# Four changes of order in the first half of a fused four-layer kernel: GpSimd's order by hand, the variance, the top-k rounds and two dense tiles

## The chip, the cores and the metric

The kernel is one program on one core of one Trainium2 chip. The metric is device time in microseconds (us) of that core, from one launch to its end; the figure for a kernel is the median over runs. Before the change three runs gave 838.84, 840.29 and 840.7 us, so a median of 840.29.

A core has five engines that run side by side, each with its own queue: TensorE (matrix products, PE in the profile), VectorE (DVE), ScalarE (ACT), GpSimd (POOL) and SyncE (SP), which here only starts transfers. An engine takes its instructions strictly in the order of its queue. One that waits for another engine holds up everything behind it.

## The reference, cut to what matters

The input x has 4 x 256 tokens of 256 values; ctx_512 has 4 x 256 rows of 64. Each of four layers adds a gated attention and a gated feed-forward part to x. The change touches layer 0, the attention of layer 1, and two things that are computed there ahead of time for later use: the ternary weights of layer 1's feed-forward part and the adjacency of layer 2.

```python
def _L0_xattn_ref(p, k_v, W_k, b_k, ln_gamma, ln_beta):
    kv = k_v @ W_k.T + b_k
    out = jnp.einsum('bij,bjd->bid', p, kv)
    sim = jnp.einsum('bid,bjd->bij', out, kv) * 256 ** (-0.5)
    mu = jnp.mean(sim, axis=-1, keepdims=True)
    var = jnp.var(sim, axis=-1, keepdims=True)
    sim = (sim - mu) * jax.lax.rsqrt(var + EPS) * ln_gamma + ln_beta
    return jax.nn.softmax(sim, axis=-1)

def _L0_ffn_ref(x, gate_w, gate_b, expert_w, expert_b):
    gate_logits = jnp.einsum('nsd,de->nse', x, gate_w) + gate_b
    _, top_idx = jax.lax.top_k(gate_logits, 2)                  # 2 of 8 experts
    all_out = jax.nn.relu(jnp.einsum('nsd,edo->nseo', x, expert_w) + expert_b)
    return jnp.take_along_axis(all_out, top_idx[..., None], axis=2).mean(axis=2)

# layer 1: causal softmax attention with 16 heads of 16 over keys from ctx_512;
# its feed-forward part rounds three 1024 x 256 weights to -1, 0 or 1:
def weight_quant(w):
    scale = 1.0 / jnp.clip(jnp.mean(jnp.abs(w)), EPS)
    return jnp.clip(jnp.round(w * scale), -1.0, 1.0) / scale

# layer 2's attention matrix comes from ctx_512 alone; k = 76 of 256
topk_vals = jax.lax.top_k(sim, k)[0]
sparse_mask = (sim >= topk_vals[:, :, -1:]).astype(sim.dtype)
A_learned = jax.nn.sigmoid(sim) * sparse_mask
A_learned = (A_learned + jnp.swapaxes(A_learned, -1, -2)) * 0.5

x = x + jnp.tanh(g_xattn[0]) * _L0_xattn_ref(_layernorm(x), ctx_512, ...)
x = x + jnp.tanh(g_ffn[0]) * _L0_ffn_ref(_layernorm(x), ...)
x = x + jnp.tanh(g_xattn[1]) * _L1_xattn_ref(_layernorm(x), ctx_512, ...)
...
```

## The kernel before, in words

**Tiles.** The 1024 tokens are eight tiles of 128 rows, which stay on chip all the time; a half is four tiles, two batch entries. A layernorm works on one half (`layernorm`, L173): statistics on VectorE, the power -0.5 of the variance on GpSimd (L183, ln_rstd), then four normalizations on VectorE (L187, xn). `transposed` (L193) turns the half on TensorE (L199) and copies it out (xnT, L109 when VectorE does it). `evac` (L105) gives such copies to VectorE and ScalarE by turns. `project` (L206) is the common matmul of projections and routing.

**The order.** Most of the kernel leaves the order of instructions to a scheduler. Up to the end of layer 1's attention TensorE's order is that of the source text (`in_order`, L217, opened at L444), and so are ScalarE's and VectorE's (L588 to L590, closed at L1034). GpSimd's is the scheduler's. SyncE starts the loads, each when its buffer is free. Matmuls write to eight PSUM banks that `bank` hands out in turn, so that an operation may have to wait until an earlier reader has left its bank.

**Layer 0, attention (L592 to L718).** For each half: the similarities (L634) on TensorE, with and without the layernorm's gain, their squares summed on ScalarE (L649, s_drop), the variance from them on VectorE (L654, s_ve) and its power on GpSimd (L656), then `softmax0` (L659: scaling at L660, maxima, Exp) and the gated addition `add0` (L680). The first half's normalization and the second half's similarities are interleaved; the routing of the first half ends the stage.

**Layer 0, feed-forward (L762 to L823).** All eight experts are computed for every token and multiplied by 0 or 0.5. `dense` does one tile: four banks, a bias matmul in each (L766), the experts' matmuls (L772), eight ReLUs on ScalarE that scale by the routing weight (L780, into buffers re, of which there are three), and the sum over experts on GpSimd (L785, L786). `add_mean` (L789) adds the result to x on VectorE. The loop runs over tiles 0 to 5; tile 6 and 7 are done in steps 0 and 1 of the next stage. Beside the tiles stand pieces of other work:

- top-k rounds for layer 2. A row's 76th largest value is found by ten rounds; each takes the eight largest (L479) and strikes them out (L482), the tenth applies the threshold (L486). There are 8 x 10 = 80 rounds, all on VectorE. `graph_rows(n)` (L493) puts the next n in the queue.
- keys and values of layer 1 (`keys1`, L516; `values1`, L531).
- four pieces for each of the three ternary weights (L549 to L571): `ternary_sum` of absolute values (ScalarE), `ternary_mean` (a matmul and three small operations on VectorE, L558 to L562), `ternary_scale` (L566 on ScalarE, L567 on VectorE) and `ternary_round` (ScalarE). The raw weights come through the same ten load buffers as the experts' weights.
- after tile 4, the layernorm of the first half for layer 1; the second half's is in step 3 of the attention.

**Layer 1, attention (L854 to L1033).** Per batch entry a query projection (`Maxima`, L206 with wq) and four steps that find each row's maximum (scores on TensorE, L885 m on VectorE, then two small operations and `late`, which adds the maxima to the queries); one batch entry later four steps (`Sums`) that compute exp(score - maximum) on ScalarE, multiply by the values, transpose (oT) and divide, then `turn` (attT) and `output` with the residual addition. So there are 20 steps and 5 more to drain; steps 4 to 15 do both kinds, steps 16 to 19 only sums. Top-k rounds and, from step 20 on, the transposition of the adjacency (`graph_batch`, L497) stand in these steps. Then follows layer 1's feed-forward part, whose first operation on VectorE is the quantization of its input (L1161).

How tiles, rounds and steps were written:

```python
means[t] = dense(t % HT, *((xt0, counts0) if t < HT else (xt1, counts1)))
graph_rows(3)
if t:
    add_mean(t - 1)
if t == 4:
    tiles = layernorm(0)
graph_rows((2, 6, 6, 6, 2, 4)[t])          # the loop, t = 0 to 5
...
if n < 2:                                  # the steps, n = 0 to 24
    means[6 + n] = dense(2 + n, xt1, counts1)
    add_mean(5 + n)
...
graph_rows(5 if n < 2 else 2)
```

## Time and profile before

| | us | what it is |
|---|---|---|
| median of three runs | 840.29 | without a profile |
| the profiled execution | 829.3 | one execution, recorded |
| its span | 827.6 | first to last instruction; 1.7 lies around it |
| PE, matmuls | 707.5 | 85% of the span |
| PEld, weight loads | 426.7 | 52%, beside matmuls |
| DVE | 510.6 | 62% |
| ACT | 283.3 | 34% |
| POOL | 212.2 | 26% |

The mean granted clock of TensorE in this execution is 0.914 of full speed. The profiled execution is shorter than each of the three runs, so sums over it are made against its own 829.3.

The parts of the span, with the time that the engines are busy in each and the clock (the parts that the prediction shows are left out):

| part of the span | what runs | length | PE | DVE | clock |
|---|---|---|---|---|---|
| 0 to 40.5 | loads, layer 0's attention, first half | 40.5 | 25.4 | 28.0 | 0.87 |
| 40.5 to 61.0 | its second half, first routing | 20.5 | 14.3 | 14.6 | 0.75 |
| 61.0 to 102.7 | dense tiles 0 to 4 | 41.7 | 41.7 | 35.0 | 0.92 |
| 262.3 to 360.0 | layer 1's feed-forward part | 97.7 | 73.6 | 80.1 | 0.92 |
| 360.0 to 827.6 | layers 2 and 3 | 467.6 | 424.5 | 234.0 | 0.94 |

Between them lie 102.7 to 123.9 (tile 5 and the layernorm for layer 1), 123.9 to 173.0 (dense tiles 6 and 7 with steps 0 to 3), 173.0 to 241.4 (steps 4 to 15) and 241.4 to 262.3 (the last steps).

How to read the lines that follow. In the busy slices each digit is the busy share of one of 40 equal slices in tenths. A line of waits says which instruction waits (engine, tile, line), what released it, and then total, number and longest of the waits in us. A line of the timeline begins with its time and its duration, both in us, then engine, line, operation, what is written and from what, the shape, and how many such instructions stand together; a bracket gives the wait ahead of it and what ended it. A line of windows gives a stretch, its length, each engine's busy time with its number of instructions, the clock, the share of the transfer engines and GB/s.

### The profile page before, as it was taken

The page shows a single profiled execution, that of the slowest core. Times are in us where ns is not written, and L with a number is a line of the kernel's source. Part 1 is how long each engine was busy: PE and PEld are TensorE (multiplying, and loading weights), DVE is VectorE, ACT ScalarE, POOL GpSimd, SP SyncE. Part 2 cuts the span into 40 slices and gives each one's busy share as a digit, 9 for nine tenths or more (in the row PEclk, how much of TensorE's full clock was granted, in tenths as well). Part 3 has the DMA queues.
Part 4 walks back from the last instruction along what each step waited for, and adds up shares of the span by engine and source line. Part 5 has one row for each costly group of instructions (what it writes and reads, how often), then busy time and mean ns, then how long its engine had stood idle before and what let it go on. Part 6 is the DMA issues. An engine that isn't in the chain of part 4 may idle for free.

```text
span 827.6 us, 11378 instructions
## 1 busy us (share of the span) xinstructions
PE 707.5 (85%) x4121; PEld 426.7 (52%) x4121; DVE 510.6 (62%) x1398; ACT 283.3 (34%) x583; POOL 212.2 (26%) x254
## 2 busy tenths in 40 slices
PE   5679939669989689729999997999998979989996
PEld 3434415446655367516477746654543325547754
DVE  6778883879885789864314455887777524213334
ACT  2444632423233143213103310156554655013320
POOL 4123352100000334210544362100000010733334
PEclk9778978779999799967999999899999998989998
DMA  8700111110000000000258833200000000369933
GB/s 256 252 0 1 38 38 30 49 37 2 20 2 8 13 1 1 0 0 1 85 182 284 271 95 108 84 1 2 1 1 2 1 1 0 113 238 333 341 108 109
DMA packets 32848, 64.35 MB, mean 78 GB/s; under 512 B 5180, under 2 KB 22488, under 8 KB 32536
## 3 DMA queue, kind: packets, MB, share of 16 engines
q1 hardware_dynamic: 24136, 31.47, 11.6%
q0 software_dynamic: 8224, 31.76, 11.5%
q8 instruction: 33, 0.54, 0.3%
q10 hardware_dynamic: 432, 0.39, 0.2%
q14 instruction: 23, 0.19, 0.1%
HBM read 49.31 MB, written 14.30 MB: 77 GB/s over the span
## 4 chain that ended last, share of the span: by engine, by line
PE 59%; DVE 19%; issue 10%; DMA 4%; ACT 4%; POOL 3%; SPq 0%; ACTq 0%; DVEq 0%; POOLq 0%
PE b L206 21%; PE b L772 6%; PE b L399 6%; PE b L1290 4%; PE b L1305 3%; PE b L1259 3%; PE b L347 3%; PE b L1106 3%; DVE pad L1266 3%; DMA d_w<-in_ffn_r_dram,d_of 2%; DVE xn L187 2%; POOL ln_rstd L183 2%; DVE x L372 2%; DVE g_work L482 1%; ACT pT L1297 1%
## 5 line engine op out<-in xcount | busy, mean ns | idle before, releaser
L206 PE MATMUL b<-xnT,w 128*128 128x512 f32 (+2 forms) x288 | 119.9, 574 | 10.4 <-DVE xnT L109 10.4
L1266 DVE TENSOR_REDUCE pad<-b 128x2 f32<-128x512 f32 x128 | 80.9, 684 | 20.7 <-PE b L1290 20.3
L206 PEld LDWEIGHTS b<-xnT,w 128*128 128x128 f32 (+1 forms) x288 | 56.3, 200 | 66.1 <-issue 62.5
L1297 ACT ACTIVATE pT<-b 128x512 f32<-128x512 f32 x128 | 68.7, 598 | 50.7 <-PE b L1290 50.7
L1259 PE MATMUL b<-kT,qT 32*128 32x256 f32 x512 | 71.8, 417 | 3.2 <-DVE pad L1266 3.2
L1290 PE MATMUL b<-qm,kT 32*128 32x512 f32 x256 | 73.6, 649 | 0.0
L312 POOL DMA_INDIRECT d_w<-in_ffn_r_dram,d_of x46 | 43.8, 952 | 109.1 <-PE b L319 61.5
L206 PE MATMUL b<-d_w,d_xT 128*128 128x256 f32 (+1 forms) x184 | 58.0, 439 | 2.8 <-DMA d_w<-in_ffn_r_dram,d_of 1.7
L772 PE MATMUL b<-w,xnT 128*128 128x512 f32 x128 | 59.9, 623 | 0.0
L1259 PEld LDWEIGHTS b<-kT,qT 32*128 32x128 f32 x512 | 41.7, 191 | 33.3 <-DVE pad L1266 10.9
L399 PE MATMUL b<-w,hT 128*128 128x256 f32 x224 | 53.9, 395 | 2.0 <-DVE hT L385 2.0
L785 POOL TENSOR_TENSOR re<-re 128x512 f32<-128x512 f32 (+1 forms) x32 | 32.4, 1015 | 75.1 <-ACT re L780 73.9
L384 ACT ACTIVATE sil<-b 128x512 f32<-128x512 f32 (+1 forms) x28 | 16.7, 597 | 99.7 <-PE b L206 99.7
L399 PEld LDWEIGHTS b<-w,hT 128*128 128x128 f32 x224 | 42.3, 195 | 15.0 <-issue 6.9
L385 DVE TENSOR_TENSOR hT<-b,sil 128x512 f32<-128x512 f32 (+1 forms) x28 | 19.3, 688 | 45.9 <-ACT sil L384 45.9
L183 POOL TENSOR_TENSOR ln_rstd<-ln_ve,neghalf 128x4 f32<-128x4 f32 x16 | 16.3, 1019 | 120.1 <-DVE ln_ve L181 120.0
L925 ACT ACTIVATE pT<-b 128x384 f32<-128x384 f32 x64 | 26.2, 497 | 53.7 <-PE b L919 53.7
L1106 PE MATMUL b<-had,zT 128*128 128x256 f32 x128 | 33.8, 421 | 10.3 <-ACT hwork L1117 7.2
L199 PE MATMUL b<-ident,xn 128*128 128x128 f32 x80 | 17.4, 359 | 29.1 <-DVE xn L187 28.0
L187 DVE TENSOR_SCALAR xn<-x,ln_mv,ln_rstd 128x256 f32<-128x256 f32 x64 | 26.5, 468 | 24.5 <-POOL ln_rstd L183 24.5
L772 PEld LDWEIGHTS b<-w,xnT 128*128 128x128 f32 x128 | 24.9, 200 | 31.0 <-issue 31.0
L885 DVE TENSOR_REDUCE m<-b 128x3 f32<-128x384 f32 x64 | 31.1, 547 | 13.9 <-PE b L879 13.9
(278 smaller groups left out, 1319.4 us busy)
## 6 DMA issues: line engine op xcount, KB each, us to landing
d_x<-rows_in SPq DMA_DIRECT2D x46, 128.0 KB, 4.4
rows_out<-d_y SPq DMA_DIRECT2D x46, 128.0 KB, 4.7
w<-in_ffn_s_dram SPq DMA_DIRECT2D x13, 384.0 KB, 3.5
w<-in_l_w_dram SPq DMA_DIRECT2D x6, 512.0 KB, 4.6
rows_in<-zero SPq DMA_DIRECT2D x1, 2944.0 KB, 14.3
w<-in_expert_w_dram SPq DMA_DIRECT2D x4, 512.0 KB, 5.6
x<-in_x_dram SPq DMA_DIRECT2D x8, 128.0 KB, 3.6
kT<-in_l_kT_dram SPq DMA_DIRECT2D x1, 1024.0 KB, 4.9
```

What stands on the lines that cost most here:

```text
L183: nc.gpsimd.tensor_tensor(rstd, ve, neghalf, ALU.pow)
L187: nc.vector.tensor_scalar(xn, x[h * HT + i], mv[:, i, 0:1], rstd[:, i : i + 1], ALU.subtract, ALU.mult)
L206: nc.tensor.matmul(dst, lhs(kc), rhs(kc), start=kc == 0, stop=kc == KC - 1)
L312: nc.gpsimd.indirect_dma_start(out=w, out_offset=None, in_=src, in_offset=self.indices(self.of[:, n : n + 1]))
L399: nc.tensor.matmul(po, hT[:hs, j, i * P : (i + 1) * P], w[:hs, 4 * hs : 4 * hs + D], start=j == 0, stop=j == len(ws) - 1,)
L772: nc.tensor.matmul(pe, xt[:, kc, i * P : (i + 1) * P], ws0[j][:, kc * 2 * D : (kc + 1) * 2 * D], start=False, stop=kc == KC - 1,)
L785: nc.gpsimd.tensor_add(re[:, :n, :], re[:, :n, :], re[:, n : 2 * n, :])
L1106: nc.tensor.matmul(pf[:, c // 2, (c % 2) * 2 * P : (c % 2 + 1) * 2 * P], self.zT[:, c0 : c0 + P], had2[:, n].rearrange("p s q -> p (s q)") ...
L1259: nc.tensor.matmul(pn[:, half * S : (half + 1) * S], self.qT[group(k), ah, g0 + half, qt * P : (qt + 1) * P], kT[group(k), ah, self.b * S ...
L1266: nc.vector.tensor_reduce(self.pads[qt][:, ah, g0 : g0 + 2, k, D3], pn.rearrange("p (g s) -> p g s", g=2), AX.X, ALU.max, negate=True,)
L1290: nc.tensor.matmul(pn, kT[group(k), ah, c : c + P], self.qm[group(k), ah, g0 : g0 + 2, :], start=True, stop=True)
L1297: nc.scalar.activation(self.pT[u][:, k, :], pn, AF.Exp, scale=D3**-0.5)
```

## The change

It leaves every operation in place and changes their order; the number of instructions of each engine is the same before and after.

- GpSimd's order becomes that of the source text too, for the same stretch as the others'. With it, the sum over experts is taken out of `dense` into a function of its own, `sum_up`, which stands after the statistics and the power for the layernorm in tile 4.
- The variance of the first attention's similarities is taken out of `similarities` into `factors`. For the second half it is called after `layernorm(0)`.
- The loads of the first raw ternary weight stand ahead of the experts' weights in SyncE's queue.
- The loop over tiles is unrolled: `ffn_tile(t, rounds, early)` does a tile, its sum, its rounds and its ternary pieces; keys and values follow in `part_of_keys(t)`. The pieces of the third ternary weight move from steps 2 to 4 of the attention to tiles 5 to 7.
- Dense tiles 6 and 7 leave steps 0 and 1: tile 6 stands ahead of the first query projection, tile 7 behind it, both ahead of step 0.
- The 80 rounds are placed anew. Tiles 0 to 5 had 5, 9, 9, 9, 5 and 7, steps 0 and 1 had 5 each, later ones 2. Now tiles 0 to 7 have 5, 9, 9, 8, 3, 7, 4 and 7, steps 0 to 3 none, steps 4 to 15 one each, and steps 16 to 19 four each. `graph_batch` moves one step later.

```diff
--- before.py
+++ after.py
@@ -154,6 +154,7 @@
     nc.sync.dma_start(rbias[:, 1, :], a["expert_bias"].partition_broadcast(P))
     ebias = const.tile([16, P], F32, tag="ebias", name="ebias")
     nc.sync.dma_start(ebias, a["expert_b"].rearrange("(p f) -> p f", p=16))
+    raw = [[weights(a["l1_w0"][j], FF1) for j in range(2)]]
     ws0 = [weights(a["expert_w"][j], KC * 2 * D) for j in range(E // 2)]
     had = const.tile([P, P], F32, tag="had", name="had")
     nc.sync.dma_start(had, a["hadamard"])
@@ -588,6 +589,7 @@
     all_orders = ExitStack()
     all_orders.enter_context(in_order(ACT))
     all_orders.enter_context(in_order(mybir.EngineType.DVE))
+    all_orders.enter_context(in_order(mybir.EngineType.Pool))
     with tc.tile_pool(name="l0a", bufs=1) as lp:
         tiles0 = layernorm(0)
         pk = bank()
@@ -650,11 +652,15 @@
                         drop[:, :S], sims[0][i][:, it, :], AF.Square,
                         accum_out=square[:, 2 * i + it : 2 * i + it + 1],
                     )
+            return sims[1], square
+
+        def factors(square):
             ve = sm([HT], "s0_ve")
             nc.vector.tensor_scalar(ve, square, 1.0 / (S * 256.0), 1e-6, ALU.mult, ALU.add)
             rstd = sm([HT], "s0_rstd")
             nc.gpsimd.tensor_tensor(rstd, ve, neghalf, ALU.pow)
-            return sims[1], rstd
+            return rstd
+
 
         def softmax0(pss, rstd, between=lambda: None):
             nc.vector.tensor_scalar_mul(rstd, rstd, 1.0 / 16.0)
@@ -699,21 +705,23 @@
         for j in range(E // 2):
             nc.sync.dma_start(eb[32 * j : 32 * j + 3, :], eb_parts[:, j * 2 * D : (j + 1) * 2 * D])
 
-        held = similarities(0, out_of(0, xt))
+        pss, square = similarities(0, out_of(0, xt))
+        rstd = factors(square)
         nc.scalar.activation(gates, gates, AF.Tanh)
         xt = transposed(tiles1)
         qkT2 = lp.tile([P, 2, 2, S], F32, tag="qkT2", name="qkT2")
         oT = []
-        weighted = softmax0(*held, lambda: oT.append(out_of(1, xt)))
+        weighted = softmax0(pss, rstd, lambda: oT.append(out_of(1, xt)))
         graph_projections(qkT2)
-        held = similarities(1, *oT)
+        pss, square = similarities(1, *oT)
         add0(0, *weighted)
         tiles0 = layernorm(0)
+        rstd = factors(square)
         graph_scores(0, qkT2)
         graph_scores(1, qkT2)
         xt0 = transposed(tiles0)
         pl = route(xt0, 0, E)
-        weighted = softmax0(*held)
+        weighted = softmax0(pss, rstd)
         counts0 = choose(pl)
         add0(1, *weighted)
 
@@ -780,9 +788,12 @@
                 nc.scalar.activation(
                     re[:, e % 4, :], pe[:, (e % 2) * D : (e % 2 + 1) * D], AF.Relu, scale=counts[:, i, e : e + 1]
                 )
-            if j % 2:
-                for n in (2, 1):
-                    nc.gpsimd.tensor_add(re[:, :n, :], re[:, :n, :], re[:, n : 2 * n, :])
+        return means
+
+    def sum_up(means):
+        for re in means:
+            for n in (2, 1):
+                nc.gpsimd.tensor_add(re[:, :n, :], re[:, :n, :], re[:, n : 2 * n, :])
         nc.gpsimd.tensor_add(means[0][:, 0, :], means[0][:, 0, :], means[1][:, 0, :])
         return means[0][:, 0, :]
 
@@ -791,36 +802,50 @@
 
     tiles1 = layernorm(1)
     wq = weights(a["l1_wq"], KC * 4 * P)
-    raw = [[weights(a[f"l1_w{n}"][j], FF1) for j in range(2)] for n in range(3)]
+    raw += [[weights(a[f"l1_w{n}"][j], FF1) for j in range(2)] for n in (1, 2)]
     means = {}
-    for t in range(NT - 2):
-        if t == 1:
-            pl = route(xt1, 0, E)
-        means[t] = dense(t % HT, *((xt0, counts0) if t < HT else (xt1, counts1)))
-        if t == 0:
-            nc.scalar.activation(
-                graph.rearrange("p t s -> p (t s)"), gsim.rearrange("p t s -> p (t s)"), AF.Sigmoid,
-                scale=1.0 / 16.0,
-            )
+
+    def ffn_tile(t, rounds, early=lambda: None):
+
+        parts = dense(t % HT, *((xt0, counts0) if t < HT else (xt1, counts1)))
         graph_rows(3)
-        if t == 1:
-            counts1 = choose(pl)
+        early()
         if t:
             add_mean(t - 1)
-        if t == 4:
-            tiles = layernorm(0)
-        graph_rows((2, 6, 6, 6, 2, 4)[t])
-        if t == 0:
-            xt1 = transposed(tiles1)
-        if t < HT:
-            keys1(t)
-            values1(*divmod(t, 2))
+        if t == HT:
+            tiles1.extend(layernorm(0))
+        means[t] = sum_up(parts)
+        graph_rows(rounds)
         for when, piece, n in (
             (0, ternary_sum, 0), (1, ternary_mean, 0), (1, ternary_scale, 0), (2, ternary_sum, 1),
             (2, ternary_round, 0), (3, ternary_mean, 1), (3, ternary_scale, 1), (4, ternary_round, 1),
+            (5, ternary_sum, 2), (6, ternary_mean, 2), (6, ternary_scale, 2), (7, ternary_round, 2),
         ):
             if t == when:
                 piece(n)
+
+    def part_of_keys(t):
+        keys1(t)
+        values1(*divmod(t, 2))
+
+    ffn_tile(0, 2)
+    nc.scalar.activation(
+        graph.rearrange("p t s -> p (t s)"), gsim.rearrange("p t s -> p (t s)"), AF.Sigmoid, scale=1.0 / 16.0
+    )
+    xt1 = transposed(tiles1)
+    part_of_keys(0)
+    pl = route(xt1, 0, E)
+    chosen = []
+    tiles1 = []
+    ffn_tile(1, 6, lambda: chosen.append(choose(pl)))
+    counts1, = chosen
+    part_of_keys(1)
+    ffn_tile(2, 6)
+    part_of_keys(2)
+    ffn_tile(3, 5)
+    part_of_keys(3)
+    ffn_tile(4, 0)
+    ffn_tile(5, 4)
 
 
 
@@ -989,24 +1014,16 @@
         with ExitStack():
             steps = 4 * (B + 1)
             plan = [([], []) for _ in range(steps + 5)]
-            xt = transposed(tiles)
+            ffn_tile(6, 1)
+            xt = transposed(tiles1)
             mx, sums, following = Maxima(0, xt), None, None
+            ffn_tile(7, 4)
+            add_mean(7)
+            in_l0f.close()
             for n in range(steps + 5):
                 b, j = divmod(n, 4)
-                if n < 2:
-                    means[6 + n] = dense(2 + n, xt1, counts1)
-                    add_mean(5 + n)
-                elif n == 2:
-                    add_mean(7)
-                    in_l0f.close()
-                    ternary_sum(2)
-                elif n == 3:
-                    ternary_mean(2)
-                    ternary_scale(2)
-                elif n == 4:
-                    ternary_round(2)
-                elif steps <= n < steps + B:
-                    graph_batch(n - steps)
+                if steps < n:
+                    graph_batch(n - steps - 1)
                 if j == 0 and 0 < n <= steps:
                     sums = Sums(b - 1, mx.qT) if n < steps else None
                     mx, following = following, None
@@ -1022,7 +1039,7 @@
                     if j == 3:
                         plan[n + 2][1].append(sums.turn)
                         plan[n + 3][1].append(sums.output)
-                graph_rows(5 if n < 2 else 2)
+                graph_rows(0 if n < 4 else 1 if n < 16 else 4)
                 for todo in plan[n][1]:
                     todo()
                 if n == 3:
```

## What was predicted

> **What bounds the kernel now.** I read the busy slices first, then TensorE's waits, then stage windows, then the timeline at each wait. The slices (20.7 us each):
>
> ```profile
> PE   5679939669989689729999997999998979989996
> DVE  6778883879885789864314455887777524213334
> PEclk9778978779999799967999999899999998989998
> ```
>
> TensorE is nearly full from slice 9 to the end of the attention and is hollow in slices 0 to 2, 5, 7 and 8; VectorE is high just there. TensorE's longest waits up to 300 us (total, times, longest) name it:
>
> ```profile
> PE b L199 <- DVE xn L187: 17.7, 8, 5.7
> PE b L206 <- DVE xnT L109: 11.7, 3, 8.4
> PE b L848 <- DVE m L885: 6.5, 6, 3.3
> ...
> PE b L897 <- DVE m L885: 3.4, 1, 3.4
> ```
>
> So the stretch from 0 to 173 us is set by VectorE's queue. The stages (length; busy time of PE, weight loads, DVE, ACT, POOL; clock):
>
> ```profile
> 102.70:123.90 21.20, 8.17 (x23) 3.62 (x21) 18.97 (x52) 7.76 (x18) 10.61 (x11) 0.72 0.13 37
> 123.90:173.00 49.10, 38.33 (x200) 21.97 (x200) 30.69 (x94) 17.27 (x33) 10.44 (x11) 0.78 0.16 49
> 173.00:241.40 68.40, 60.86 (x708) 40.58 (x708) 58.44 (x182) 20.06 (x49) 1.01 (x1) 0.97 0.02 7
> 241.40:262.30 20.90, 20.78 (x205) 12.78 (x204) 10.84 (x39) 9.06 (x23) 0.00 (x0) 0.92 0.01 2
> ```
>
> Read: VectorE full in the first row, TensorE full in the last, where VectorE has 10.06 us free. The points that the change touches, from the timeline:
>
> ```profile
> 28.02 0.17 DVE L654 TENSOR_SCALAR s_ve<-s_sq 128x4 f32<-128x4 f32 x1 [3.05 <-ACT s_drop L649]
> ...
> 52.56 1.01 POOL L183 TENSOR_TENSOR ln_rstd<-ln_ve,neghalf 128x4 f32<-128x4 f32 x1
> ...
> 53.61 1.78 DVE L187 TENSOR_SCALAR xn<-x,ln_mv,ln_rstd 128x256 f32<-128x256 f32 x4 [4.96 <-POOL ln_rstd L183]
> ...
> 109.82 4.14 POOL L785 TENSOR_TENSOR re<-re 128x512 f32<-128x512 f32 x4
> 109.89 4.22 DVE L187 TENSOR_SCALAR xn<-x,ln_mv,ln_rstd 128x256 f32<-128x256 f32 x4 [1.13 <-POOL ln_rstd L183]
> ...
> 123.85 6.37 PE L206 MATMUL b<-xnT,w 128*128 128x256 f32 x16 [8.36 <-DVE xnT L109]
> ```
>
> Read: VectorE held 3.05 us by a variance that could wait, then 4.96 us by an rstd behind GpSimd adds; the query projection held until VectorE has done its top-k rounds.
>
> **What the Trainium skill says.** "SBUF — State Buffer", Who interferes with whom: VectorE's tensor_scalar in a two-port mode and a GpSimd operation exclude each other for a whole instruction. The trace agrees: four xn take 4.22 us beside the adds above, and 1.38 us at 33.70 with GpSimd idle. "TensorE: Matmul & The Clock Gate", What's actually happening: after an idle window the clock is half until some microseconds of work. The trace agrees: the projection's 16 matmuls take 6.37 us after the 8.36 us wait, 3.69 us at 182.44. "Perfetto Trace Analysis", Optimization Strategy: a gap that repeats on the saturated engine can mean that SBUF or PSUM has no room for the next tile. Before, no dense tile waits for a bank; I use it for the changed kernel below.
>
> **The change, part by part.** A top-k round (L479 with L482) takes 0.98 us (55.32 to 56.29). Times in the changed kernel are "new".
>
> Start. The variance goes behind the other half's normalization, so VectorE takes the reciprocal when its Exps are done (25.5) instead of at 28.09: 2.5 us. The constants' memsets leave the first normalization: its four xn, 2.02 us beside them, take 1.38: 0.6. They now run from about 33 to 37, where only a 128x4 multiply (L660) can meet them: 0 to 0.7 us, I take 0. onesb is ready at 33.4, first used at 38. The zero memset moves to about 35, and SP's zeroing transfer waits for it at the queue's head; behind it SP has only loads that themselves wait until 87, so nothing. Two 512 KB loads for the ternary weights go ahead of the experts' on SP: at 334 GB/s (10 to 20 us) 3.1 us later, landing about 22 for a use at 38: nothing. Sum 3.1.
>
> The rstd. It now stands ahead of the adds: of the 4.96 us wait 1.1 stays (the pow itself), 3.9 goes. ln_ve (1.07 us beside an add at 47.58, else 0.17) gives 0.9. But the adds now run beside xn: 1.78 us becomes between 1.4 and 4.2; I take 3.6, loss 1.8. ScalarE's two Abs passes (2.1 us) move ahead of the sigmoid and of its half of xnT: that half is ready at 54.1, VectorE's at about 54.7, so they cost nothing by 0.6 us. Sum 3.0; the second routing starts at 54.8 (60.93 before).
>
> Tiles 1 to 3. TensorE and VectorE move together. The ternary pieces ahead of the keys' evictions save VectorE's wait for them in tile 1, 0.6; one round less in tile 3, 1.0. VectorE reaches tile 4 at 102.8-6.1-1.6 = 95.1. New wait: with the ternary mean ahead of the keys, the built program's dense tile 4 takes its fourth bank from that mean, which VectorE reads (L560) at about 90.6; TensorE is ready at 87.5. It stands 3.1 us with everything behind it; ScalarE's relus and then GpSimd's adds wait for that. VectorE is later still, so I count nothing.
>
> Tiles 4 to 6, VectorE's queue. Tile 4: 3 rounds 2.95, add 0.5, statistics 2.3, rstd 1.1, xn 4.2 (GpSimd's adds of tile 4 now stand behind that rstd, so they collide again) = 11.05, to 106.2. Tile 5: 7 rounds and an add, 7.4, to 113.6. Tile 6: 4 rounds 3.9, add 0.5, mean and scale 0.7, wait for ScalarE 1.25, two L567 with a gap 1.8, to 121.7; xnT 0.7. The projection starts at 122.5, only 1.3 earlier, but dense tile 6 is already behind it. TensorE idles some 8 us before it, as now.
>
> To step 4's maxima (L885 at 173.00). Projection to 128.9 at half clock, dense tile 7 to 136.4 (7.1). VectorE does 7 rounds and an add by 135.4, then waits for tile 7's mean: last relu 137.2, adds 2.1 and 0.7, then 0.5: 140.6. Four steps of maxima 1.95, copies 0.33, late add 0.41: 10.8; two qT copies 0.8; a wait of 2 behind the second projection (3.7 on TensorE); the second normalization 2.3, 1.1, 1.4: 4.8. Sum 159.0: 14.0 us earlier.
>
> Steps 4 to 15 take one round instead of two (until step 14). TensorE's waits for VectorE between 174 and 241 are 2.08, 0.33, 0.18, 0.24, 1.05, 2.01 = 5.9; TensorE is otherwise full. Between 1 and 5.9 can go; the last hides an rstd, so I take 3.5. The maxima of step 15 (240.6) come at 223.1.
>
> Steps 16 to 19 take four rounds each. With the one of step 15 that is 17 x 0.98 = 16.7 us into 10.06 free: 6.7 us over. They stand in order ahead of oT, attT and the residual adds, for which TensorE waits, and ahead of the next stage's xq (262.28). Bound: 0 if TensorE's tail stretches anyway, 8.4 if VectorE also waits there. I take 6.7; xq comes at 251.5. The batch transposes move one step later, the same four of 0.6 and 0.7.
>
> The sum: 14.0 + 3.5 - 6.7 = 10.8, say 11 us. The later stages keep their order. The profiled execution took 829.3 (span 827.6 and 1.7 around it), so 818.3 for it; the median shown is 840.29, 1.3% above, so 829.3.
>
> **The rivals.** Tail hidden: VectorE is already free at step 16 and the rounds fill gaps. For it: TensorE is 89% busy in steps 5 to 15 and VectorE loses 11 us there. Against: 16 rounds in 16 us of four steps leave no gap. Gain 17.5: 822.8.
>
> Small gain: the xn collide fully (0.6 more), the steps give 1, the tail costs 8.4. For it: the 4.22 us xn. Against: all three at once. About 14.0-0.6+1-8.4 = 6, and less if tile 4 slips by a few: 835.
>
> Slower: GpSimd's fixed order at tile 4. The three re buffers tie the tiles: relu(t+1) waits for a buffer, that for add_mean(t) on VectorE, that for GpSimd's adds, which wait behind an rstd that waits for VectorE. If each of tiles 4 to 7 costs 3.4 us more, the projection starts at 136, step 4 gains 0.5, and the tail outweighs it: +2.7, 843.0. It decides from a projection start of 133.3 on (gain then 3.2 + 3.5 = 6.7). For it: ScalarE waits for GpSimd once already, 0.46 us at 108.76. Against: in my sum each mean is ready when VectorE asks, but for tile 7.
>
> That the orders don't come out as written: the built program has them as the diff says.
>
> **How the numbers follow.** The forecast (gain 7 to 15) 0.50, tail hidden 0.15, small gain (1.7 to 7) 0.17, no change 0.05, slower 0.13. What a measurement can tell from no change is 0.2%, 1.7 us. Faster 0.82, same 0.05, slower 0.13. The range 821.5 to 838.5 takes in the first three.
>
> **What would show it.** Right: L654's 3.05 us wait gone; the second routing near 55; L199's wait at the second half short; the projection at 122 to 123 after a wait of some 8 us; a stop of TensorE of about 3 us ahead of dense tile 4; step 4's maxima near 159; VectorE nine tenths or more in the last four steps, and TensorE waiting there for oT or attT; xq near 251. Wrong: the projection after 130 (GpSimd's order costs), VectorE with gaps in steps 16 to 19 (tail hidden), or the later stages changing length.

## The result, and the profile after

The changed kernel takes 829.98 us, median of four runs (826.62 to 831.49), beside 840.5 (838.84 to 841.97) for the kernel before: a ratio of 0.987, 95% interval 0.9832 to 0.9908. It is 10.5 us faster. The forecast was 829.3, in a range of 821.5 to 838.5.

The profiled execution does not show that at first sight. Its span is 829.4 us, against 827.6 in the profile before. The stages do. All lines L... from here on are those of the kernel that is shown; in the changed one most of them have moved down by 1 to 25. The windows of the changed kernel, from dense tile 4 on, cut at the query projection, step 4's maxima, step 15's maxima and the first transposition of layer 1's feed-forward part (length; PE, weight loads, DVE, ACT, POOL; clock):

```profile
87.00:121.90 34.90, 26.49 (x72) 11.29 (x70) 29.40 (x83) 19.50 (x37) 17.74 (x21) 0.88 0.07 23
121.90:160.10 38.20, 29.82 (x178) 19.05 (x178) 21.66 (x67) 9.66 (x19) 5.73 (x6) 0.81 0.20 62
160.10:222.50 62.40, 59.81 (x705) 40.87 (x706) 48.32 (x150) 20.07 (x49) 1.01 (x1) 0.96 0.03 8
222.50:255.10 32.60, 25.13 (x234) 16.98 (x234) 29.80 (x103) 11.40 (x25) 1.39 (x3) 0.95 0.00 1
255.10:829.40 574.30, 498.15 (x2665) 305.28 (x2662) 309.59 (x769) 179.96 (x356) 156.67 (x177) 0.92 0.26 86
```

and of the kernel before, cut at the same events, from the projection on:

```profile
123.80:173.00 49.20, 38.38 (x200) 22.05 (x200) 30.69 (x94) 17.27 (x33) 10.44 (x11) 0.78 0.16 49
173.00:240.60 67.60, 60.65 (x705) 40.57 (x706) 57.64 (x181) 20.06 (x49) 1.01 (x1) 0.97 0.02 7
240.60:267.60 27.00, 25.39 (x233) 16.47 (x233) 16.23 (x53) 11.28 (x25) 1.40 (x3) 0.94 0.01 1
...
267.60:827.60 560.00, 493.59 (x2665) 301.79 (x2663) 309.49 (x770) 180.28 (x356) 157.16 (x177) 0.93 0.26 88
```

Read: layer 1's feed-forward part begins at 255.1 instead of 267.6, so 12.5 us are gained in the part that the change touches. The steps 0 to 3 with the projection fall from 49.2 to 38.2 (one dense tile stands there now instead of two), steps 4 to 15 from 67.6 to 62.4; the last steps grow from 27.0 to 32.6, with VectorE busy for 29.8 of them instead of 16.2. Then the same code, with nearly the same busy times, takes 574.3 instead of 560.0. That has to be settled first.

TensorE's waits in the first 300 us of the changed kernel (total, times, longest):

```profile
PE b L207 <- DVE xnT L109: 8.1, 2, 4.9
PE b L200 <- DVE xn L188: 5.7, 4, 2.3
...
PE b L922 <- DVE cm L916: 4.4, 2, 3.8
PE b L922 <- DVE m L910: 4.2, 1, 4.2
PE b L774 <- DVE mw L561: 3.6, 1, 3.6
```

The waits for normalized tiles are down from 17.7 to 5.7 and those for xnT from 11.7 to 8.1. L774 is new: the bias matmul of dense tile 4, which waits for a bank that the ternary mean holds. The points of the timeline that the prediction named:

```profile
44.65 1.01 POOL L184 TENSOR_TENSOR ln_rstd<-ln_ve,neghalf 128x4 f32<-128x4 f32 x1 [8.56 <-DVE ln_ve L182]
...
45.63 2.07 POOL L796 TENSOR_TENSOR re<-re 128x512 f32<-128x512 f32 x2
...
45.69 3.77 DVE L188 TENSOR_SCALAR xn<-x,ln_mv,ln_rstd 128x256 f32<-128x256 f32 x4 [1.13 <-POOL ln_rstd L184]
```

Read: the power now comes ahead of the adds and VectorE waits 1.13 us for it, not 4.96; the four multiplications then run beside those adds and take 3.77 us. The last sign that the prediction named is xq, VectorE's first operation for layer 1's feed-forward part. It had put it near 251.5:

```profile
248.02 1.28 DVE L1178 TENSOR_SCALAR xq<-xn 128x256 bf16<-128x256 f32 x4
...
249.84 0.55 PE L995 MATMUL b<-ident,att 128*128 128x128 f32 x3 [3.11 <-DVE att L984]
```

Read: xq comes 3.5 us before its forecast (249.0 in the second profile), 14.3 us earlier than the 262.28 of the kernel before. But it stands ahead of the attention's last divisions (att), for which TensorE waits 3.11 us, and TensorE's first transposition in the feed-forward part comes 7.0 us behind xq instead of 5.4. The tables below use that transposition.

### The profile page after: what moved, and what is told of

It reads as the page before. It is cut to its first block, busy times and chain, and to the rows that moved or that the text cites. A ratio compares the mean times of both kernels' runs of the same rounds, so it can differ in the third digit from the quotient of the medians.

```text
span 829.4 us, 11375 instructions
## 1 busy us (share of the span) xinstructions
PE 710.8 (86%) x4121; PEld 430.5 (52%) x4121; DVE 510.3 (62%) x1398; ACT 283.1 (34%) x583; POOL 212.0 (26%) x254
## 4 chain that ended last, share of the span: by engine, by line
PE 44%; DVE 15%; another core or an unknown queue 4%; ACT 3%; DMA 3%; issue 2%; POOL 1%; SPq 0%; ACTq 0%; DVEq 0%; POOLq 0%
PE b L207 18%; PE b L400 5%; PE b L1307 4%; PE b L1123 4%; DVE pad L1283 4%; PE b L1322 3%; PE b L348 3%; PE b L1276 3%; DMA d_w<-in_ffn_r_dram,d_of 2%; ACT pT L1314 1%; DVE x L373 1%; PE b L320 1%; DVE xn L188 1%; DVE z L1097 1%
## 5 line engine op out<-in xcount | busy, mean ns | idle before, releaser
L207 PE MATMUL b<-xnT,w 128*128 128x512 f32 (+2 forms) x288 | 123.4, 588 | 5.3 <-DVE xnT L109 4.9
L207 PEld LDWEIGHTS b<-xnT,w 128*128 128x128 f32 (+1 forms) x288 | 58.7, 208 | 62.3 <-issue 52.3
L780 PE MATMUL b<-w,xnT 128*128 128x512 f32 x128 | 64.0, 658 | 0.0
L400 PE MATMUL b<-w,hT 128*128 128x256 f32 x224 | 57.1, 409 | 8.0 <-issue 4.6
L1276 PEld LDWEIGHTS b<-kT,qT 32*128 32x128 f32 x512 | 43.4, 198 | 33.1 <-DVE pad L1283 10.5
L385 ACT ACTIVATE sil<-b 128x512 f32<-128x512 f32 (+1 forms) x28 | 16.6, 597 | 119.0 <-PE b L207 73.4
L207 PEld LDWEIGHTS b<-d_w,d_xT 128*128 128x128 f32 x184 | 32.1, 194 | 15.7 <-ACT d_xT L111 3.7
L365 POOL DMA_INDIRECT d_yt<-rows_out,d_row x32 | 30.5, 954 | 36.8 <-DMA rows_out<-d_y 24.4
## 6 DMA issues: line engine op xcount, KB each, us to landing
d_x<-rows_in SPq DMA_DIRECT2D x46, 128.0 KB
rows_out<-d_y SPq DMA_DIRECT2D x46, 128.0 KB
x<-in_x_dram SPq DMA_DIRECT2D x8, 128.0 KB
```

The lines of the kernel that those rows point to most:

```text
L207: nc.tensor.matmul(dst, lhs(kc), rhs(kc), start=kc == 0, stop=kc == KC - 1)
L365: nc.gpsimd.indirect_dma_start(out=y, out_offset=None, in_=rows_out, in_offset=self.indices(self.at[:, n, t : t + 1]))
L400: nc.tensor.matmul(po, hT[:hs, j, i * P : (i + 1) * P], w[:hs, 4 * hs : 4 * hs + D], start=j == 0, stop=j == len(ws) - 1,)
L780: nc.tensor.matmul(pe, xt[:, kc, i * P : (i + 1) * P], ws0[j][:, kc * 2 * D : (kc + 1) * 2 * D], start=False, stop=kc == KC - 1,)
L1276: nc.tensor.matmul(pn[:, half * S : (half + 1) * S], self.qT[group(k), ah, g0 + half, qt * P : (qt + 1) * P], kT[group(k), ah, self.b * S ...
```

## The experiments

Twelve runs followed, in three groups of four; the runs of one group, with the kernel before beside them, share a chip. Two of them repeat the kernels before and after. The table has, for each profile, the times of five events in us (second routing, query projection, step 4's maxima, step 15's maxima, first transposition of layer 1's feed-forward part), the rest of the span from there, then the median and the ratio to the kernel before, with its interval.

| kernel | routing | projection | step 4 | step 15 | feed-forward | rest | median | ratio |
|---|---|---|---|---|---|---|---|---|
| before | 60.9 | 123.8 | 173.0 | 240.6 | 267.6 | 560.0 | 840.5 | 1 |
| before_again | 61.7 | 124.6 | 174.2 | 241.8 | 268.8 | 574.0 | 841.56 | 0.9997 [0.9978, 1.0016] |
| after | 55.0 | 121.9 | 160.1 | 222.5 | 255.1 | 574.3 | 829.98 | 0.987 [0.9832, 0.9908] |
| after_again | 55.7 | 123.8 | 159.6 | 223.4 | 257.0 | 575.8 | 830.28 | 0.9863 [0.9813, 0.9914] |
| no_pool_order | 59.2 | 127.7 | 164.7 | 228.4 | 262.0 | 567.7 | 836.53 | 0.9951 [0.9929, 0.9972] |
| variance_back | 59.9 | 128.0 | 163.8 | 227.6 | 261.2 | 571.1 | 834.12 | 0.9922 [0.9891, 0.9953] |
| ternary_late | 54.4 | 124.5 | 162.0 | 225.8 | 259.9 | 573.9 | 833.63 | 0.9913 [0.9884, 0.9942] |
| rounds_undone | 54.3 | 122.3 | 167.5 | 235.1 | 261.9 | 573.7 | 836.8 | 0.9947 [0.9927, 0.9966] |
| dense_in_steps | 54.2 | 114.1 | 153.4 | 216.0 | 248.7 | 570.5 | 823.45 | 0.9806 [0.9766, 0.9845] |
| no_late | 54.1 | 122.4 | 160.5 | 222.9 | 249.7 | 572.5 | 823.23 | 0.9799 [0.9758, 0.9841] |
| sum_first | 55.2 | 125.4 | 163.7 | 226.1 | 258.7 | 560.5 | 821.02 | 0.9893 [0.9848, 0.9939] |
| free1 | 54.2 | 121.1 | 158.8 | 222.6 | 256.2 | 557.8 | 817.86 | 0.9871 [0.9832, 0.991] |
| free2 | 55.3 | 111.7 | 153.9 | 216.9 | 243.7 | 558.1 | 803.68 | 0.9697 [0.9658, 0.9735] |
| free3 | 54.9 | 110.1 | 146.4 | 210.3 | 237.1 | 561.0 | 800.14 | 0.965 [0.9603, 0.9696] |

In the last group (sum_first, free1 to free3) the kernel before took 829.33 us, in the others 840.94 and 841.8, so medians are compared through their ratios alone. Two profiles of one kernel differ by up to 1.9 us at an event.

**Where the 14 us of the later part went.** The kernel before, unchanged.

> The kernel before once more, unchanged. In the first pair of profiles the changed kernel begins layer 1's feed-forward part at 255.1 us instead of 267.7 (12.6 earlier), but from there to the end of its span it takes 574.4 us instead of 560.0, though that code is the same. Theory A (the part after layer 1's attention varies by itself from one execution to the next): this profile begins the feed-forward part at 267.7 within 0.5 again, but takes 565 to 577 us from there, not 560. Theory B (the change lengthens the later part): 560 within 3 again. The time itself: 840 within 3 in both.

Measured: 268.8, which is 1.1 later than 267.7 and not within 0.5, and then 574.0 us. So the kernel before has the long rest too, as theory A said. The table shows more: the rest is 568 to 576 us in every profile of the first two groups, and 558 to 561 in the last group and in the first profile of the kernel before, whatever the kernel. So it goes with the group, not, as theory A said, from one execution to the next, and not with the change. The place where it starts can be read: before layer 2's first routed expert TensorE waits on this

```profile
PE b L399 <- issue: 4.1, 3, 1.7
```

in the kernel before's second profile (the third matrix product of the shared part of layer 2's feed-forward; it waits for nothing that the profile shows). The nine profiles with the long rest have 3.7 to 5.0 us of it, the five with the short rest none. The first routed expert comes 172.2 to 172.9 us after the start of layer 1's feed-forward part in the profiles of the kernels before and after with the long rest, and 164.3 to 165.3 in the five with the short one: 8 of the 14 us lie there. What makes it so was not tried. The forecast took its gain from the median and not from the profile's 829.3, so the short rest of that one profile did it no harm.

> The changed kernel once more, unchanged, beside the others. Theory A (the first 255 us repeat, the later part varies by itself): layer 1's feed-forward part begins at 255.1 within 1.2 (the two profiles of the kernel before differ by 1.2 there), from there to the end 560 to 577 us, and the ratio to the kernel before is 0.987 within 0.003. Theory B (the change lengthens the later part): never under 572 from there.

Measured: 257.0 (1.9 later, not within 1.2), 575.8 and 0.9863. The 575.8 alone would fit theory B as well; against B speaks that the kernel before has 574.0, and that sum_first and free1, two small variants of the changed kernel, have 560.5 and 557.8. Over two profiles each, the feed-forward part begins at 256.1 instead of 268.2, 12.1 us earlier.

**GpSimd's order.** The edit:

```diff
-    all_orders.enter_context(in_order(mybir.EngineType.Pool))
```

> The changed kernel with GpSimd's order left to the scheduler again. Theory (VectorE's wait for a power behind the adds is worth 3 us at the second routing, and again some in tile 4): the second routing at 58 or later instead of 55.0, layer 1's feed-forward part begins 3 to 5 us later than 255.1, and the time is 0.3 to 0.6% above the changed kernel's 829.98. Rival (with the sums taken out of the dense tiles the scheduler finds the same order by itself): the second routing at 55.0 within 0.5 and no difference. Second rival (the fixed order costs in tile 4): the feed-forward part begins earlier than 254.

Measured: 59.2, and a feed-forward part at 262.0, 5 to 7 us later; 0.9951 against 0.987. The theory holds and its figure was too small. GpSimd and VectorE in this run:

```profile
48.85 2.07 POOL L795 TENSOR_TENSOR re<-re 128x512 f32<-128x512 f32 x2 [0.98 <-ACT re L787]
50.87 1.02 POOL L184 TENSOR_TENSOR ln_rstd<-ln_ve,neghalf 128x4 f32<-128x4 f32 x1
...
51.93 1.78 DVE L188 TENSOR_SCALAR xn<-x,ln_mv,ln_rstd 128x256 f32<-128x256 f32 x4 [6.53 <-POOL ln_rstd L184]
...
108.67 3.21 DVE L188 TENSOR_SCALAR xn<-x,ln_mv,ln_rstd 128x256 f32<-128x256 f32 x4 [3.60 <-POOL ln_rstd L184]
```

Read the brackets: 6.53 us at the first place, 3.60 in tile 4, where the changed kernel waits 1.13 and 1.14. The scheduler does not find this order by itself, although the sums stand apart in the source. In tile 4 the kernel before had it, with a wait of 1.13 us for the power: it is in the rewritten source that the scheduler loses it there. So 5 to 7 us is what the fixed order is worth within the changed kernel, not what it gained over the kernel before.

**The variance.** The edit puts `factors` back ahead of the additions:

```diff
         pss, square = similarities(1, *oT)
+        rstd = factors(square)
         add0(0, *weighted)
         tiles0 = layernorm(0)
-        rstd = factors(square)
```

> The changed kernel with the variance of the second half's similarities in its old place, ahead of the additions and the normalization. Theory (VectorE's queue carries the delay to the second routing and on to the query projection): the second routing 2 to 2.5 us later than 55.0, the query projection as much later than 121.9, and layer 1's feed-forward part begins 2 to 2.5 us later than 255.1. Rival (a later wait swallows it, that of 4.9 us ahead of the query projection first): the second routing later by 2, the projection and what follows by less than 0.7.

Measured: the routing 4.2 to 4.9 us later, the projection 4.2 to 6.1, the feed-forward part likewise 4.2 to 6.1. The delay is carried through undiminished, as the theory has it. It is larger than expected, since VectorE now waits

```profile
28.72 0.17 DVE L659 TENSOR_SCALAR s_ve<-s_sq 128x4 f32<-128x4 f32 x1 [3.81 <-ACT s_drop L651]
```

3.81 us instead of the 3.05 of the kernel before (why it is more was not tried), and the first xn run beside the constants' memsets again (1.95 us instead of 1.38).

**The new stall of TensorE.** The ternary pieces of tiles 1 to 3 go behind the keys and values again:

```diff
-            if t == when:
+            if t == when and (t in (0, 4, 5, 6, 7)):
                 piece(n)
...
     def part_of_keys(t):
         keys1(t)
         values1(*divmod(t, 2))
+        for when, piece, n in (
+            (1, ternary_mean, 0), (1, ternary_scale, 0), (2, ternary_sum, 1),
+            (2, ternary_round, 0), (3, ternary_mean, 1), (3, ternary_scale, 1),
+        ):
+            if t == when:
+                piece(n)
```

> The changed kernel with the ternary pieces of tiles 1 to 3 behind the keys and values again, so that dense tile 4's fourth bank no longer waits for the ternary mean (TensorE stood 3.6 us there). Theory (VectorE is later still, so that stall costs nothing): the stall is gone, but the query projection starts at 121.9 within 1 (up to 0.6 later, since VectorE waits for its evictions in tile 1 again), after a wait that is about 3 us longer than 4.9. Rival (the stall holds up everything behind it): the projection 2.5 to 3.6 us earlier.

Measured: the stall is gone and the wait ahead of the projection is 11.1 us instead of 4.9. The projection comes at 124.5, 0.7 to 2.6 later. So the stall of 3.6 us costs nothing that shows, as forecast: in the changed kernel VectorE never waits for TensorE between dense tile 4 and the projection. What the pieces' place gains was sized too low: VectorE waits 2.84 us for the keys in tile 1 here, and not 0.6, and the feed-forward part begins 2.9 to 4.8 us later.

**The rounds.** All 80 in their old places:

```diff
-        graph_rows(3)
+        graph_rows(3 if t < 6 else 0)
...
-                graph_rows(0 if n < 4 else 1 if n < 16 else 4)
+                graph_rows(5 if n < 2 else 2)
```

and tiles 3, 4, 6 and 7 with 6, 2, 0 and 0.

> The changed kernel with the 80 top-k rounds where they were before (tiles 6 and 7 have none, steps 0 and 1 five each, later steps two each until step 14). Theory (VectorE sets steps 0 to 3; TensorE most of steps 4 to 15; VectorE steps 16 to 19 with the late rounds): step 4's maxima at 169 instead of 160.1 (14 rounds of 0.98 us instead of 7 that stood beside dense tile 7, less 5 us of gaps), step 15's at 235 instead of 222.5, the last part 5.5 us shorter, so layer 1's feed-forward part begins at 262 instead of 255.1 and the time is 0.8% above the changed kernel's. Rival (what the first steps gain the last ones give back): 255.1 within 1.5.

Measured: 167.5, 235.1, and 26.8 us for the last part (261.9 less 235.1), so 261.9. The theory holds at each event within 1.5 us; the rounds' new places are worth 5 to 7 us, 0.8% in the ratios.

> The changed kernel without the 16 top-k rounds of steps 16 to 19: the last tile and a half of layer 2's adjacency are left without their threshold. Theory (VectorE sets the last steps): from step 15's maxima to the start of layer 1's feed-forward part 27 us, as in the kernel before, instead of 32.6, so it begins at 249.6 instead of 255.1. Rival (the late rounds fill gaps, and the stretch is longer for another reason): 255.1 within 1.

The edit is `graph_rows(0 if n < 4 else 1 if n < 16 else 0)`. Measured: 249.7. The last part:

```profile
222.90:249.70 26.80, 24.36 (x234) 15.93 (x234) 16.56 (x57) 11.28 (x25) 1.39 (x3) 1.00 0.01 2
```

26.8 us instead of 32.6, with TensorE's work nearly unchanged and VectorE's 29.8 us of work down to 16.6. The sixteen late rounds cost 5.8 us.

**The dense tiles.** Tiles 6 and 7, with all that belongs to them, in steps 0 and 1 again:

```diff
-            ffn_tile(6, 1)
             xt = transposed(tiles1)
             mx, sums, following = Maxima(0, xt), None, None
-            ffn_tile(7, 4)
-            add_mean(7)
-            in_l0f.close()
             for n in range(steps + 5):
                 b, j = divmod(n, 4)
+                if n < 2:
+                    ffn_tile(6 + n, (1, 4)[n])
+                elif n == 2:
+                    add_mean(7)
+                    in_l0f.close()
```

> The changed kernel with dense tiles 6 and 7, their rounds and ternary pieces in steps 0 and 1 again. Theory (the 11 us between the projection and step 4 come from the rounds taken out of the steps, not from where the dense tiles stand): the projection starts near 113 instead of 121.9, since 4 rounds, an addition and the ternary mean and scale no longer stand ahead of it, but step 4's maxima come within 2 us of 160.1 and layer 1's feed-forward part within 2 of 255.1. Rival (dense tiles and scores in each other's way, for banks or for VectorE, are what cost): the feed-forward part begins at 259 or later.

Measured: the projection at 114.1, as expected, and then neither theory. Step 4's maxima come at 153.4 and the feed-forward part at 248.7, 6.4 to 8.3 us earlier than in the changed kernel; 0.9806 against 0.987. Each of its runs (820.86 to 824.42) is below each run of the changed kernel on the same chip (825.29 to 834.5). This part of the change is a loss. The windows of this run from dense tile 4 to step 4:

```profile
87.20:114.10 26.90, 19.18 (x51) 8.20 (x49) 22.98 (x64) 14.07 (x27) 13.32 (x16) 0.87 0.09 30
114.10:153.40 39.30, 33.79 (x200) 19.44 (x200) 27.61 (x86) 15.13 (x29) 11.18 (x11) 0.94 0.21 61
```

66.2 us together, against 73.1 (34.9 + 38.2). VectorE does nearly the same work, 50.6 us here and 51.1 in the changed kernel; the difference is its waits. Those from the projection to step 4, of the changed kernel and then of this one:

```profile
DVE qT L109 <- PE b L207: 8.1, 3, 3.0
DVE x L373 <- POOL re L797: 4.9, 1, 4.9
DVE m L910 <- PE b L904: 1.7, 1, 1.7
```

```profile
DVE qT L109 <- PE b L207: 4.2, 2, 2.4
DVE mw L561 <- PE b L559: 3.9, 1, 3.9
```

Read: with the tiles apart from the steps, VectorE has no other work placed ahead of its waits for tile 7's mean (4.9) and for both projections, whose results it copies (8.1); the second profile has 4.7 and 6.0. In the steps, tile 7's seven rounds stand between two maxima, and the wait for its mean is gone. A part of the difference in the projections is TensorE's own pace. The second one, in the changed kernel and then here:

```profile
142.78 6.19 PE L207 MATMUL b<-xnT,w 128*128 128x256 f32 x16
...
137.08 2.75 PE L207 MATMUL b<-xnT,w 128*128 128x256 f32 x12
140.44 1.13 PE L207 MATMUL b<-xnT,w 128*128 128x256 f32 x4 [0.61 <-DVE m L910]
```

In the changed kernel it follows a wait of TensorE of 3.8 us and takes 6.19 us (5.30 in the second profile). Here a dense tile of 7.1 us stands shortly ahead of it, and the same sixteen matmuls take 3.88. The clock granted from the projection to step 4 is 0.94 here and 0.81 there. The edit moves the tiles, their rounds and the pieces of the third ternary weight together; which of them carries how much of the 6.4 to 8.3 us was not separated.

**Filling the wait.** Four rounds from tile 5 to tile 7, in the changed kernel: `ffn_tile(5, 0)` and `ffn_tile(7, 8)`.

> The changed kernel with four top-k rounds moved from tile 5 to tile 7, where VectorE waits 4.9 us for tile 7's mean. Theory (the stretch from tile 4 to step 0 is as long as VectorE's work plus its own waits there: 4.9 for the mean, 5.2 in the first projection): the projection starts 3.9 us earlier, near 118 to 120, step 0's maxima too, and layer 1's feed-forward part at 251 to 253. Rival (TensorE's dense tiles set it): the feed-forward part within 1 of 255 to 257.

Measured: the projection at 121.1, the feed-forward part at 256.2, ratio 0.9871. My theory failed. The feed-forward part comes where the rival had put it, but not for the rival's reason, for VectorE does not wait for TensorE between tile 4 and the projection. What stands ahead of the projection in this run:

```profile
115.58 0.28 PE L559 MATMUL b<-w_sum,ones 128*128 128x2 f32 x2
```

```profile
109.95 1.47 DVE L373 SCALAR_TENSOR_TENSOR x<-re,gates,x 128x256 f32<-128x256 f32 x1
...
114.75 0.94 DVE L373 SCALAR_TENSOR_TENSOR x<-re,gates,x 128x256 f32<-128x256 f32 x1
...
116.47 0.15 DVE L561 TENSOR_REDUCE mw<-b 128x1 f32<-128x2 f32 x1
...
118.28 2.17 DVE L568 TENSOR_SCALAR w<-w 128x1024 f32<-128x1024 f32 x2 [1.16 <-ACT w L567]
```

and the first of the two additions in the changed kernel:

```profile
108.96 0.47 DVE L373 SCALAR_TENSOR_TENSOR x<-re,gates,x 128x256 f32<-128x256 f32 x1
```

Read: the matmul for the third ternary weight's mean ends at 115.86, and VectorE takes the mean (L561) at 116.47 straight from a round, without a wait. From the start of tile 4's xn to the projection it takes 18.1 us, against 19.9 and 19.7 in the changed kernel: 1.6 to 1.8 less, not 3.9. With the four rounds gone, the two additions to x now fall beside GpSimd's adds and take 1.47 and 0.94 us instead of 0.47 and 0.48. Little more was to be had there, since the mean comes from TensorE only behind dense tile 6, 0.6 us before VectorE asks for it. The four rounds fit nearly into tile 7's wait, as meant: from the projection to step 0's maxima it takes 17.9 us instead of 18.1 and 16.9. What is left of the gain lies within the 1.9 us by which two profiles of one kernel differ. So moving these four rounds does not repair what the dense tiles' place costs.

**Tile 4's order on GpSimd**, the slower rival's mechanism, in one place: `sum_up` ahead of the rounds and the statistics for tile 4 alone.

> The changed kernel with tile 4's sum over experts ahead of the power on GpSimd, as plain source order would have it (only there). Theory: the power waits for the adds, which end when the last ReLU has, at about 105 instead of 102, but the four xn then stand beside no add and take 1.4 us instead of 4.25; the query projection and layer 1's feed-forward part begin 0 to 1.5 us later than in the changed kernel (121.9 to 123.8 and 255.1 to 257.0 in its two profiles). Rival (GpSimd's fixed order in tile 4 is what decides this stretch): 3.4 us or more later.

Measured: the power at 105.21, VectorE's wait 5.24 us, the four xn 2.92, and the feed-forward part at 258.7: 1.7 to 3.6 later, between theory and rival; ratio 0.9893 against 0.987, intervals that overlap. So the direction is that of the changed kernel's order, and the size stays open.

**A better version.** free2 takes dense_in_steps, moves tile 5's four rounds to tile 6 and puts rounds into the gaps of the projections; free3 also takes four rounds from tile 7 and splits the second normalization. Of the two edits:

```diff
+                gaps = ((1, 0, 2, 0, 0), (0, 0, 0, 0, 0), (1, 0, 1, 0, 1), (1, 0, 1, 0, 1))[b]
                 for j in range(4):
+                    graph_rows(gaps[j])
                     pq = bank()[:, :S]
...
-                if n == 3:
-                    tiles = layernorm(1)
+                if n == 2:
+                    parts1 = statistics(1)
+                if n == 3:
+                    tiles = normalized(1, *parts1)
```

> Dense tiles 6 and 7 in steps 0 and 1 as in the run that gained by it, and rounds moved to where VectorE waits: tile 5's four to tile 6, three into the first query projection, six into those of batch entries 2 and 3, so that seven are left for steps 16 to 19. Theory: the projection at 110.5 instead of 114.1, step 4's maxima at 150 instead of 153.4, the last part 3 us shorter, layer 1's feed-forward part at 242 instead of 248.7, ratio to the kernel before 0.973. Rival (the gaps are there because TensorE is late for another reason, and the rounds in the projections hold up their copies): 247 or later.

> As the run before, and tile 7's last four rounds go to steps 16 to 19 (eleven there), and the statistics of the second half's normalization stand in step 2 and its four multiplications in step 3, so that the power is waited for behind maxima. Theory: TensorE's 4.2 us wait ahead of step 4 goes, the last part is 1.4 us longer, layer 1's feed-forward part begins at 239 to 240. Rival (the wait goes but VectorE's work catches up in the next steps): 241 to 242, no better than the run before.

Measured: free2 reaches the projection at 111.7, but step 4 at 153.9, no gain over dense_in_steps there; the last part is 5.9 us shorter (26.8 for 32.7) and the feed-forward part begins at 243.7, where the theory had 242. free3:

```profile
110.10:146.40 36.30, 31.98 (x192) 18.50 (x196) 31.63 (x94) 15.39 (x30) 13.42 (x16) 0.97 0.23 66
...
210.30:237.10 26.80, 24.27 (x233) 15.95 (x233) 25.41 (x88) 11.28 (x25) 1.40 (x3) 1.00 0.01 2
```

TensorE's wait of 4.2 us ahead of step 4 is gone, step 4 comes at 146.4, and the feed-forward part begins at 237.1, earlier than the theory's 239 to 240. The eleven rounds left for the last steps fit there: VectorE is busy for 25.4 of 26.8 us and the part is no longer than with none. It takes 800.14 us against 829.33, a ratio of 0.965 (0.9603 to 0.9696), where the changed kernel has 0.987.

## Why the prediction was right

| term of the sum | predicted | measured (two profiles) |
|---|---|---|
| start: TensorE's dense tile 0 earlier than 40.5 | 3.1 | 3.2, 3.0 |
| second routing | 54.8 | 55.0, 55.7 |
| four xn beside the adds | 3.6 | 3.77 in the first |
| VectorE's first round in tile 4 | 95.1 | 95.19 in the first |
| TensorE's stop ahead of dense tile 4 | 3.1 | 3.6, 3.6 |
| query projection | 122.5 | 121.9, 123.8 |
| step 4's maxima | 159.0 | 160.1, 159.6 |
| steps 4 to 15, shorter by | 3.5 | 5.2, 3.8 |
| step 15's maxima | 223.1 | 222.5, 223.4 |
| last steps up to the first transposition, longer by | 6.7 | 5.6, 6.6 |
| last steps up to xq, longer by | 6.7 | 3.9, 3.9 |
| xq | 251.5 | 248.0, 249.0 |
| gain: xq earlier by | 11 | 14.3, 14.5 |
| gain: first transposition of the feed-forward part earlier by | 11 | 12.5, 11.8 |
| gain: medians | 11 | 10.5 |

At 40.5 us TensorE begins dense tile 0. The table of the parts of the span, ahead of the prediction, gives 40.5 to 61.0 to the attention's second half; that is what VectorE does there, while TensorE does dense tile 0 and, from 61.0 on, the second routing and tiles 1 to 4.

The sum came out because VectorE's queue was walked in its new order, event by event, with the waits in it, from the start to step 4; up to step 15 each event lies within 1.4 us of its forecast. The undone parts show that this queue is indeed what carries time: with the variance back in its place, some 4.5 us lost by the second routing are 4.2 to 6.1 lost at the end. The gain of the start was a little larger (3.2), the wait ahead of the projection smaller (4.9 and 4.3 instead of some 8), since TensorE came there later than I had put it, after its stop and 9.77 us for dense tile 4.

The last term was read at another event than it was forecast for. At xq the last steps are longer by 3.9 us, not 6.7; the late rounds delay the work that stands behind xq as well, and at the first transposition 5.6 to 6.6 are reached. That the medians come within half a microsecond of the forecast is in part luck, since single terms are off by up to 3 us.

Two readings within the sum were wrong or missing, though they did not show in it. The prediction gave one figure, 14.0 us, for all that comes before step 4, and counted the dense tiles' move as a help there ("dense tile 6 is already behind it"). That move alone costs 5 us by the ratios and 6 to 8 by the profiles, and the rounds' new places gain about what it loses. And it priced GpSimd's order at the second routing alone (3.0). As a change from the kernel before that is right for tile 4, where the wait was 1.13 us already; it did not see that in the rewritten source the scheduler would let VectorE wait 3.60 us there, so that the fixed order is needed twice. Undone one at a time, GpSimd's order, the variance, the ternary pieces and the rounds lose about 6.0, 5.2, 3.9 and 5.9 us at the start of the feed-forward part (against the mean, 256.1), and the dense tiles gain 7.4: 13.6 in all for a change of 12.1. This is a rough agreement and no proof that the parts add up: each figure rests on one profile, within 1.9 us, and the loads of the first ternary weight were not undone alone.

Of the rivals, the hidden tail falls with no_late (5.8 us). So does the small gain: it ended at 7 us, and the end of the ratio's interval, 0.9908, is still 7.7 us. The slower one decided from a projection at 133.3 on, which comes at 121.9 and 123.8. Of the signs, VectorE is busy for nine tenths of the last steps (29.8 of 32.6 us), and TensorE waits there for att (3.3), attT (1.4) and oT (1.0). One sign of being wrong did appear, the later stages' new length (574.3 instead of 560.0), but the kernel before shows it too (574.0). What the Trainium skill says in "SBUF — State Buffer", Who interferes with whom, on VectorE's tensor_scalar and GpSimd keeping each other waiting, agrees with tile 4: the four xn take 4.25 us beside adds, 1.38 where GpSimd is idle.

## What to carry to other kernels

Walk the queue of the engine that sets a stretch in its new order, with each wait in it, and put one figure on each part of a change by walking it with that part alone left out: a right sum can hide a part that loses. A block of work that is set apart from a loop can leave the loop's waits empty, as tile 7's rounds did here; before moving it, look at which engine had used it to fill them. Taking work out of a queue can gain less than its length, if what follows then falls beside another engine's work: four rounds of 0.98 us taken out of tile 5 gained 1.6 to 1.8 us. Sixteen extra rounds in the last steps cost 5.8 us and eleven nothing: a gap in the profile has a size, and filling it is free only up to there.

## What the runs showed of the hardware

The same code after layer 1's attention took 558 to 561 us in one set of profiles and 568 to 576 in the other, for the kernel before and for its successors alike, with 8 us of it at one place and TensorE waiting there for nothing that the profile names (3.7 to 5.0 us). A difference between two single profiles, 1.8 us the wrong way here, says nothing on a change of 1% until the stages are compared.

The same sixteen matmuls of a query projection (batch entry 1) took 6.2 and 5.3 us in the changed kernel's two profiles, behind a wait of TensorE of 3.8 us in both, and 3.6 us in the first profile of the kernel before, where a dense tile stood shortly ahead of them.
